# A four-layer graph network: weight tiles regrouped by row chunk, loaded in half as many pieces, and three steps of the start and the end moved

## The chip, the cores and the metric

The kernel runs on one core of one Trainium2 chip. The metric is the device time of that core for one execution, in microseconds. The core has five engines: TensorE (matmuls and transposes; PE in the profile, its weight loads PEld), VectorE (DVE), ScalarE (ACT), GpSimd (POOL) and SyncE (SP), which here only issues transfers.

## The reference

`x` is 128 graphs of 128 nodes with 512 features, `adj` one 128 x 128 weighted adjacency matrix per graph, all in float32. Four layers follow each other, each with a residual and a layer norm:

```
x = norm(x + relu(An x W0 + b0))          An = d (A + I) d,  d = rowsum(A + I)^-1/2
x = norm(x + softmax_nodes(rowsum((q k^T / 8) * A)) * (x Wv^T))    q, k = halves of x Wqk^T
x = norm(x + relu([x, (A x) / rowsum(A)] W2^T))
x = norm(x + An (x W3 + b3))
```

The sums over a row of scores are taken without forming the scores: A k is computed and multiplied by q.

## The kernel before, in words

**Groups and layers.** The 128 graphs go in 32 groups of G = 4. A group `t` keeps its rows in the tile `x_t` (128 nodes x 4 graphs x 512) through all layers; each layer adds into it and normalizes it in place. Rows are named by `r`: r=0 stands for graphs 0 and 2, r=1 for graphs 1 and 3. All matmuls are float32.

**The 512 x 512 products.** `project` (L515 to L578) multiplies a left operand with a weight in seven products of half size instead of eight (Winograd's form of Strassen's method). In the order of TensorE they are B11, B21, T1, T2, B22, T3, T4 (layer 1 has B21 behind T1). B11, B21 use blocks of the left operand as they are; T1, T2, T3, B22 use its four sums s1 to s4 (`left_sums`: s1 is the first and s4 the last; B22 needs s4), in tiles named after the operand with an s behind, so `agg0s`, `xT1s`, `xT2s`. The weight tile holds four blocks and has three of them and the seventh slot turned into weight sums by four subtractions in place (`weight_sums`, L371 to L375). The results are put together by VectorE through `s`, `sb`, `u5`, `u2` (`u_o` and `u_v` in the profile, `s_o` and `s_v` for the copy that ScalarE makes of B11). T4 with what belongs to it is not recorded at once: it is a "tail", which `finish_tails` records, by default behind the B11 of the next `project`, so that the next product covers the waits. `hooks` are functions recorded behind a given product. PSUM has five buffers for these products (`ps_b`) and three for everything else (`ps_t`).

**Left operands.** Layers 0, 2 and 3 need the aggregate of a group transposed, which a matmul gives (`aggregate`, p_agg, copied out by ScalarE as `agg`). Layers 1 and 2 need x itself transposed (`xT`). In the steady state `turn_x` (L465 to L477) does this with DMAs: for each r two transfers into a DRAM scratch (`xT1s<-x`), four back with 32-row blocks exchanged (`xT1y<-xT1s`), and two transposes of 32 x 32 blocks by VectorE, from y into xT. `turn_on_tensor` (L479 to L491) does it with TensorE: for each graph ScalarE copies the rows in another order (into the same y buffers), TensorE transposes four 128 x 128 blocks into a PSUM buffer (`p_xT`), and ScalarE copies them to xT. The adjacency matrices: `prep_rows` (VectorE) makes row sums (`deg`), their powers (GpSimd: `d`) and the two scaled matrices (`ana`: one of x + I by d, one by the row sum); these are transposed on TensorE for groups 0 and 1 (`prep_transpose`; p_a, copied or scaled into `arT` and `anT`), and from group 2 on by DMA through DRAM (`prep_turn`: `sa<-ana`, `ya<-sa`, then VectorE's transposes into `anT`, `arT`).

**Layer 1's small operations.** `l1_qk` gives q and k for two graphs at a time (`p_qk`, copied to `qs`, `kd`), `l1_scores` A k (p_sc) and with VectorE the row sums (`scr`, `w`), `l1_softmax` transposes w (p_w), takes the maximum (`mx`) and exponential (`e`), `l1_weights` transposes back (p_ws). Norms: VectorE's statistics (bn, mv), GpSimd's `rstd` and `mr`, ScalarE's `nmr` and the scaling of x.

**Weights.** `weight` (L356 to L369) loads each of the five 512 x 512 weights (w0, wv, w2x, w2a, w3) into a tile of 128 partitions x (7 slots, 2 row chunks, 256): one transfer for each row half and each column half, so 4 of 256 KB, and with `turned`, where rows are dealt out in four blocks of 32 partitions, 16 of 64 KB.

**The order.** Everything is recorded in a `Plan` (L126 to L268) and issued by `schedule()` (L195 to L258), a list scheduler with a cost model. TensorE keeps the recorded order. VectorE, ScalarE, GpSimd and SyncE take, of what is ready by the model, what is due first, counted back from TensorE. A transfer is 470 ns of SyncE in the model and lands after 1600 ns plus its bytes over a bus. `emit` then issues all; therefore nearly all instructions of the profile stand at L266. All transfers are on SyncE's one queue, in the order of the schedule.

**The sequence.** `begin` (L829 to L851) takes group 0 through layers 0 and 1 and group 1 through layer 0. Its `l0_out(0, ...)` records group 1's adjacency transposes behind B11, and `l1_turn(1)` turns group 1's x by DMA. The main loop (L859 to L877) has, for each t and u = t - 1: l0_out(t), layer 2 of u, l0_agg(t + 1), layer 1 of t, layer 3 of u, with a new group's load and preparation. The period is 76.13 us. Behind the loop (L879 to L886) layers 2 and 3 of the last group are done in two pairs of graphs.

```
        l0_out(0, {B11: [lambda: prep_transpose(1)], B22: [lambda: l0_agg(1)]})
        ...
        l1_turn(1)
        l1_out(0, {B11: [lambda: l1_scores(0)], B21: [lambda: l1_softmax(0)], T3: []})
        finish_tails()
        for r in range(2):
            l1_qk(1, r)
        l2_both(0, 0)
```

Of the kernel before, what the change touches and what calls it, by code (L numbers as in the profile page):

```python
# [15 lines left out]
P = 128  # L16
# [109 lines left out]
class Plan:  # L126
# [4 lines left out]

    ENGINES = ("tensor", "vector", "scalar", "gpsimd", "sync")
    HOP = 200
    LAND, BUS = 1600, 95

    def __init__(self, nc, est):
        self.nc, self.est, self.ops, self.tags, self.group, self.dram = nc, est, [], {}, None, None
# [57 lines left out]
    def schedule(self):  # L195
        number = {op: i for i, op in enumerate(self.ops)}
        for (_, tag, bufs), tiles in self.tags.items():
            used = []
            for t in sorted((t for t in tiles if t.ops), key=lambda t: number[t.ops[0]]):
                if len(used) == bufs:  # L200
                    old = used.pop(min(range(bufs), key=lambda i: number[used[i].ops[-1]]))
                    assert number[old.ops[-1]] < number[t.ops[0]], (tag, bufs)
                    for op in t.ops:
                        if op.preds.isdisjoint(t.ops):
                            op.preds.update(old.ops)
                used.append(t)
        now = 0
        for op in self.ops:
            assert all(number[p] < number[op] for p in op.preds)
            for p in op.preds:  # L210
                p.succs.append(op)
            if op.engine == "tensor":
                op.last = now
                now += op.dur
        for op in reversed(self.ops):
            due = min([s.last - self.hop(op, s) for s in op.succs], default=now)
            op.last = min(op.last, due - op.dur)
        queue = {e: [] for e in self.ENGINES}
        waiting = {op: len(op.preds) for op in self.ops}
        free, bus, port = dict.fromkeys(self.ENGINES, 0), 0, 0  # L220
        pe = [op for op in self.ops if op.engine == "tensor"]
        for op in self.ops:
            if not op.preds:
                queue[op.engine].append((0, number[op], op))
        done = []
        while len(done) < len(self.ops):
            best = None
            for e in self.ENGINES:
                q = queue[e]
                if e == "tensor":  # L230
                    q = [c for c in q if c[2] is pe[0]]
                if not q:
                    continue
                q = [(max(c[0], port if c[2].port else 0),) + c[1:] for c in q]
                at = max(free[e], min(c[0] for c in q))
                pick = min((c for c in q if c[0] <= at), key=lambda c: (c[2].last, c[1]))
                for c in q:
                    if at < c[0] < at + pick[2].dur and c[2].last < at + pick[2].dur and c[2].last < pick[2].last:
                        pick, at = c, c[0]
                if best is None or at < best[0]:  # L240
                    best = at, e, pick[2]
            at, e, op = best
            queue[e] = [c for c in queue[e] if c[2] is not op]
            op.start, op.end = at, at + op.dur
            free[e] = op.end
            if op.port:
                port = op.end
            if e == "sync":
                bus = max(bus, op.end + self.LAND) + op.size / self.BUS
                op.lat = max(op.lat, bus - op.end)  # L250
            if e == "tensor":
                pe.pop(0)
            done.append(op)
            for s in op.succs:
                waiting[s] -= 1
                if not waiting[s]:
                    queue[s.engine].append((max(p.end + self.hop(p, s) for p in s.preds), number[s], s))
        return done  # L258
# [48 lines left out]
def kernel(  # L307
# [48 lines left out]
    def weight(src, name, queue, turned=False):  # L356


        w = const.tile([P, 7, 2, H], FP, tag=name, name=name)
        for h in range(2):  # L360
            for j in range(2):
                s = src[:, j * H:(j + 1) * H]
                if turned:
                    s = s.rearrange("(b h c k) m -> h b k c m", b=Q, h=2, c=2)[h]
                    for b in range(Q):
                        queue.dma_start(w[b * K:(b + 1) * K, 2 * h + j], s[b])
                else:
                    queue.dma_start(w[:, 2 * h + j], s.rearrange("(h c p) m -> h p c m", h=2, c=2)[h])
        return w  # L369

    def weight_sums(w, eng):  # L371
        eng.tensor_tensor(w[:, T3], w[:, B22], w[:, T1], ALU.subtract)
        eng.tensor_tensor(w[:, T1], w[:, T1], w[:, B11], ALU.subtract)
        eng.tensor_tensor(w[:, T2], w[:, B22], w[:, T1], ALU.subtract)
        eng.tensor_tensor(w[:, T4], w[:, B21], w[:, T2], ALU.subtract)  # L375

    def broadcast_row(src, name, queue):
        r = const.tile([P, F], FP, tag=name, name=name)
# [136 lines left out]
    def project(name, t, parts, first, c11, fin, hooks=None, after=lambda: None, early=True,  # L515
# [16 lines left out]
        def product(p, k, fresh):  # L532
            with nc.unit():
                for q in pairs:
                    for i, (left_, w) in enumerate(parts):
                        for c in range(2):
                            nc.tensor.matmul(p[:, q - pairs[0], :], operand(left_, k)[:, q, c, :], w[:, k, c, :],
                                             start=(fresh and q == pairs[0] and i == 0 and c == 0),
                                             stop=(i == len(parts) - 1 and c == 1), skip_group_check=True)
            for f in hooks.get(k, ()):  # L540
                f()
# [93 lines left out]
    def l0_agg(t, eng=nc.gpsimd, pairs=(slice(0, 2),)):  # L635
        left("agg0", t)
        for g in range(G):
            aggregate("agg0", t, g, st["anT", t])
        left_sums("agg0", t, eng, pairs)
# [189 lines left out]
    def begin():  # L829

        prep_rows(0)
        prep_transpose(0)
        weight_sums(w0_sb, nc.gpsimd)
        l0_agg(0, nc.vector, ONE_BY_ONE)
        prep_rows(1)
        l0_out(0, {B11: [lambda: prep_transpose(1)], B22: [lambda: l0_agg(1)]})
        weight_sums(wv_sb, nc.vector)
        l0_out(1)
        l1_turn(0, turn_on_tensor, (0,))
        finish_tails()  # L840
        l1_qk(0, 0)
        l1_turn(0, turn_on_tensor, (1,))
        l1_qk(0, 1)
        for w in (w2x_sb, w2a_sb, w3_sb):
            weight_sums(w, nc.gpsimd)
        l1_turn(1)
        l1_out(0, {B11: [lambda: l1_scores(0)], B21: [lambda: l1_softmax(0)], T3: []})
        finish_tails()
        for r in range(2):
            l1_qk(1, r)  # L850
        l2_both(0, 0)  # L851

    def prep(t):
# [23 lines left out]
            l2_agg(t, 0)  # L877

    l2_both(last, 0)  # L879
    for q in range(2):  # L880
        l2_out(last, {B21: [lambda: l2_both(last, 1)]} if q == 0 else {}, (q,))
    for q in range(2):
        l3_agg_pair(last, q, nc.gpsimd)
        l3_bias(last, (2 * q, 2 * q + 1))
# [34 lines left out]
```

## Time and profile before

| | |
|---|---|
| runs before | 2488.14, 2487.3, 2488.65, 2486.56 us |
| their median | 2487.72 us |
| the profiled execution | 2486.62 us, its span 2484.5 us |
| granted clock of TensorE, mean | 0.997 of full speed |
| bytes moved by DMA | 243.34 MB, mean 98 GB/s |
| loads of x, 1024 KB each | 31, median 5.3 us from issue to landing |
| loads of adj, 256 KB each | 32, median 3.6 us |
| a weight piece of w0, 256 KB | 4, median 6.4 us |

The profile is of one execution and is read in microseconds from the start of its span; the execution's own time is 2.1 us more than the span. Busy shares of the whole span say which engine is used most, and a table of stretches says where that changes. A timeline row is: start, duration, engine, line, operation, output<-inputs, shapes, the number of instructions that it sums up, and in brackets the idle time ahead of it with what ended that. A row of waits is: who waited for whom, total, times, longest. Numbers at the end of a tile's name, or before `_sb`, are left out: w0 and w3 are both `w_sb`. SPq is SyncE's queue: its time is the issuing of a transfer and not the transfer.

### The profile page before, as it was taken

The page shows a single profiled execution, that of the slowest core. Times are in us where ns is not written, and L with a number is a line of the kernel's source. Part 1 is how long each engine was busy: PE and PEld are TensorE (multiplying, and loading weights), DVE is VectorE, ACT ScalarE, POOL GpSimd, SP SyncE. Part 2 cuts the span into 40 slices and gives each one's busy share as a digit, 9 for nine tenths or more (in the row PEclk, how much of TensorE's full clock was granted, in tenths as well). Part 3 has the DMA queues.
Part 4 walks back from the last instruction along what each step waited for, and adds up shares of the span by engine and source line. Part 5 has one row for each costly group of instructions (what it writes and reads, how often), then busy time and mean ns, then how long its engine had stood idle before and what let it go on. Part 6 is the DMA issues. An engine that isn't in the chain of part 4 may idle for free.

```text
span 2484.5 us, 37083 instructions
## 1 busy us (share of the span) xinstructions
PE 2455.6 (99%) x13470; PEld 2205.1 (89%) x13470; DVE 1812.8 (73%) x3169; ACT 972.7 (39%) x1981; POOL 1335.3 (54%) x1522
## 2 busy tenths in 40 slices
PE   8899999999999999999999999999999999999998
PEld 7788988989999899889899998998898999989987
DVE  6777777777777777777777777777777777777665
ACT  3244434443334344343433443433434334443335
POOL 5456555555556465555555564645555555645443
PEclk9999999999999999999999999999999999999999
DMA  5332434433334334344333443243442434433220
GB/s 178 69 100 75 114 90 115 113 82 95 104 100 123 94 81 111 85 123 111 77 102 97 108 123 93 75 112 90 123 111 70 109 90 115 119 82 85 78 59 34
DMA packets 398805, 243.34 MB, mean 98 GB/s; under 512 B 140832, under 2 KB 365600, under 8 KB 398624
## 3 DMA queue, kind: packets, MB, share of 16 engines
q1 hardware_dynamic: 398624, 240.98, 36.4%
q8 instruction: 107, 1.75, 0.3%
q14 instruction: 74, 0.61, 0.1%
HBM read 127.66 MB, written 113.25 MB: 97 GB/s over the span
## 4 chain that ended last, share of the span: by engine, by line
PE 97%; SPq 1%; DVE 1%; DMA 1%; ACT 0%; issue 0%; POOL 0%; ACTq 0%; POOLq 0%; DVEq 0%
PE p_o L266 61%; PE p_v L266 16%; PE p_agg L266 14%; PE p_qk L266 5%; PE p_sc L266 1%; SPq L266 1%; DMA x<-in_x_dram 0%; DVE x L266 0%; PE p_ws L266 0%; ACT xT L266 0%; PE p_w L266 0%; DMA adj<-in_adj_dram 0%; PE p_xT L266 0%; ACT agg L266 0%; DVE wv_sb L266 0%
## 5 line engine op out<-in xcount | busy, mean ns | idle before, releaser
L266 ACT COPY agg<-p_agg 128x512 f32<-128x512 f32 x384 | 220.9, 583 | 572.7 <-PE p_agg L266 572.7
L266 PE MATMUL p_o<-w_sb,agg 128*128 128x256 f32 x1536 | 353.4, 379 | 0.5 <-DVE u_o L266 0.5
L266 PEld LDWEIGHTS p_o<-w_sb,agg 128*128 128x128 f32 x1536 | 286.7, 190 | 37.3 <-DVE u_o L266 0.9
L266 PE MATMUL p_o<-w2x_sb,xT2s 128*128 128x256 f32 x1024 | 263.0, 379 | 3.1 <-DVE xT2s L266 3.1
L266 PE MATMUL p_o<-w2a_sb,agg2s 128*128 128x256 f32 x1024 | 262.8, 379 | 0.0
L266 POOL TENSOR_TENSOR xT1s<-xT 128x512 f32<-128x512 f32 x64 | 94.1, 1471 | 288.0 <-DVE xT L266 190.3
L266 PE MATMUL p_agg<-anT,x 128*128 128x128 f32 x2048 | 243.9, 277 | 0.2 <-DVE anT L266 0.2
L266 PEld LDWEIGHTS p_agg<-anT,x 128*128 128x128 f32 x2048 | 235.4, 192 | 1.2 <-DVE anT L266 0.4
L266 PE MATMUL p_o<-w_sb,agg0s 128*128 128x256 f32 x1024 | 229.1, 381 | 7.2 <-DVE u_o L266 5.9
L266 PE MATMUL p_v<-wv_sb,xT1s 128*128 128x256 f32 x1024 | 233.3, 381 | 0.0
L266 POOL TENSOR_TENSOR agg3s<-agg 128x512 f32<-128x512 f32 x62 | 84.1, 1357 | 271.7 <-ACT agg L266 271.7
L266 PEld LDWEIGHTS p_o<-w_sb,agg0s 128*128 128x128 f32 x1024 | 192.9, 191 | 34.1 <-POOL mro L266 4.9
L266 PEld LDWEIGHTS p_o<-w2x_sb,xT2s 128*128 128x128 f32 x1024 | 194.4, 190 | 29.9 <-DVE xT2s L266 3.6
L266 PE MATMUL p_o<-w_sb,agg3s 128*128 128x256 f32 x992 | 219.2, 379 | 0.0
L266 PEld LDWEIGHTS p_o<-w2a_sb,agg2s 128*128 128x128 f32 x1024 | 194.6, 190 | 26.5
L266 PEld LDWEIGHTS p_v<-wv_sb,xT1s 128*128 128x128 f32 x1024 | 189.6, 190 | 27.3
L266 PEld LDWEIGHTS p_o<-w_sb,agg3s 128*128 128x128 f32 x992 | 188.5, 190 | 25.6
L266 ACT ACTIVATE x<-x,nmro,rstdo 128x512 f32<-128x512 f32 x257 | 198.7, 809 | 4.8 <-ACT nmro L266 0.3
L266 PE MATMUL p_o<-w2x_sb,xT 128*128 128x256 f32 x768 | 197.5, 380 | 1.2 <-ACT s_o L266 0.7
L266 PE MATMUL p_o<-w2a_sb,agg 128*128 128x256 f32 x768 | 197.1, 379 | 0.0
L266 DVE TENSOR_TENSOR u_o<-p_o,s_o 128x512 f32<-128x512 f32 (+1 forms) x132 | 89.1, 675 | 145.3 <-PE p_o L266 145.3
L266 PE MATMUL p_v<-wv_sb,xT 128*128 128x256 f32 x768 | 181.6, 379 | 0.9 <-DVE u_v L266 0.9
(141 smaller groups left out, 4664.1 us busy)
## 6 DMA issues: line engine op xcount, KB each, us to landing
x<-in_x_dram SPq DMA_DIRECT2D x31, 1024.0 KB, 5.3
xT1s<-x SPq DMA_DIRECT2D x124, 256.0 KB, 2.5
xT1y<-xT1s SPq DMA_DIRECT2D x248, 128.0 KB, 3.4
out_dram<-x SPq DMA_DIRECT2D x31, 1024.0 KB, 5.4
xT2s<-x SPq DMA_DIRECT2D x120, 256.0 KB, 2.6
xT2y<-xT2s SPq DMA_DIRECT2D x240, 128.0 KB, 2.9
sa<-ana SPq DMA_DIRECT2D x120, 128.0 KB, 3.3
ya<-sa SPq DMA_DIRECT2D x120, 128.0 KB, 3.3
```

The source lines that it names most:

```text
L266: getattr(getattr(self.nc, op.engine), method)(*[v.real() if isinstance(v, Ref) else v for v in args], **{k: v.real() if isinstance(v, Ref ...
```

## The change

- The weight tile is laid out as 128 partitions x (2 row chunks, 7 slots, 256), so that both column halves of a row half stand side by side and one transfer brings both: 2 transfers of 512 KB instead of 4 of 256 KB, and for `turned` 8 of 128 KB instead of 16 of 64 KB. `weight_sums` and the matmuls index accordingly; a subtraction now covers two runs of 256 elements where it had one run of 512.
- The scheduler's model lets a transfer start only when the ninth transfer before it has landed (FLIGHT). This acts on the planned order; no instruction is added.
- In `begin`, group 1's adjacency transposes are recorded behind B21 of group 0's layer 0 and not behind B11.
- In `begin`, group 1's x is turned by `turn_on_tensor` for layer 1, behind T3 of group 0's layer 1, followed by the first half of group 1's q and k; the second half stays behind the tail.
- At the end, the tail that is pending when layer 2 of the last group begins (T4 of the group before, in layer 3) is taken out of the list and recorded behind `l2_both(last, 1)`, in the B21 hook of the first pair.

```diff
--- before.py
+++ after.py
@@ -131,7 +131,7 @@
 
     ENGINES = ("tensor", "vector", "scalar", "gpsimd", "sync")
     HOP = 200
-    LAND, BUS = 1600, 95
+    LAND, BUS, FLIGHT = 1600, 95, 9
 
     def __init__(self, nc, est):
         self.nc, self.est, self.ops, self.tags, self.group, self.dram = nc, est, [], {}, None, None
@@ -222,7 +222,7 @@
         for op in self.ops:
             if not op.preds:
                 queue[op.engine].append((0, number[op], op))
-        done = []
+        done, landed = [], []
         while len(done) < len(self.ops):
             best = None
             for e in self.ENGINES:
@@ -241,6 +241,8 @@
                     best = at, e, pick[2]
             at, e, op = best
             queue[e] = [c for c in queue[e] if c[2] is not op]
+            if e == "sync" and len(landed) >= self.FLIGHT:
+                at = max(at, landed[-self.FLIGHT])
             op.start, op.end = at, at + op.dur
             free[e] = op.end
             if op.port:
@@ -248,6 +250,7 @@
             if e == "sync":
                 bus = max(bus, op.end + self.LAND) + op.size / self.BUS
                 op.lat = max(op.lat, bus - op.end)
+                landed.append(op.end + op.lat)
             if e == "tensor":
                 pe.pop(0)
             done.append(op)
@@ -356,23 +359,21 @@
     def weight(src, name, queue, turned=False):
 
 
-        w = const.tile([P, 7, 2, H], FP, tag=name, name=name)
+        w = const.tile([P, 2, 7, H], FP, tag=name, name=name)
         for h in range(2):
-            for j in range(2):
-                s = src[:, j * H:(j + 1) * H]
-                if turned:
-                    s = s.rearrange("(b h c k) m -> h b k c m", b=Q, h=2, c=2)[h]
-                    for b in range(Q):
-                        queue.dma_start(w[b * K:(b + 1) * K, 2 * h + j], s[b])
-                else:
-                    queue.dma_start(w[:, 2 * h + j], s.rearrange("(h c p) m -> h p c m", h=2, c=2)[h])
+            to = w[:, :, 2 * h:2 * h + 2].rearrange("p c j m -> p c (j m)")
+            if turned:
+                for b in range(Q):
+                    queue.dma_start(to[b * K:(b + 1) * K], src.rearrange("(b h c k) m -> h b k c m", b=Q, h=2, c=2)[h][b])
+            else:
+                queue.dma_start(to, src.rearrange("(h c p) m -> h p c m", h=2, c=2)[h])
         return w
 
     def weight_sums(w, eng):
-        eng.tensor_tensor(w[:, T3], w[:, B22], w[:, T1], ALU.subtract)
-        eng.tensor_tensor(w[:, T1], w[:, T1], w[:, B11], ALU.subtract)
-        eng.tensor_tensor(w[:, T2], w[:, B22], w[:, T1], ALU.subtract)
-        eng.tensor_tensor(w[:, T4], w[:, B21], w[:, T2], ALU.subtract)
+        eng.tensor_tensor(w[:, :, T3], w[:, :, B22], w[:, :, T1], ALU.subtract)
+        eng.tensor_tensor(w[:, :, T1], w[:, :, T1], w[:, :, B11], ALU.subtract)
+        eng.tensor_tensor(w[:, :, T2], w[:, :, B22], w[:, :, T1], ALU.subtract)
+        eng.tensor_tensor(w[:, :, T4], w[:, :, B21], w[:, :, T2], ALU.subtract)
 
     def broadcast_row(src, name, queue):
         r = const.tile([P, F], FP, tag=name, name=name)
@@ -534,7 +535,7 @@
                 for q in pairs:
                     for i, (left_, w) in enumerate(parts):
                         for c in range(2):
-                            nc.tensor.matmul(p[:, q - pairs[0], :], operand(left_, k)[:, q, c, :], w[:, k, c, :],
+                            nc.tensor.matmul(p[:, q - pairs[0], :], operand(left_, k)[:, q, c, :], w[:, c, k, :],
                                              start=(fresh and q == pairs[0] and i == 0 and c == 0),
                                              stop=(i == len(parts) - 1 and c == 1), skip_group_check=True)
             for f in hooks.get(k, ()):
@@ -833,7 +834,7 @@
         weight_sums(w0_sb, nc.gpsimd)
         l0_agg(0, nc.vector, ONE_BY_ONE)
         prep_rows(1)
-        l0_out(0, {B11: [lambda: prep_transpose(1)], B22: [lambda: l0_agg(1)]})
+        l0_out(0, {B21: [lambda: prep_transpose(1)], B22: [lambda: l0_agg(1)]})
         weight_sums(wv_sb, nc.vector)
         l0_out(1)
         l1_turn(0, turn_on_tensor, (0,))
@@ -843,11 +844,10 @@
         l1_qk(0, 1)
         for w in (w2x_sb, w2a_sb, w3_sb):
             weight_sums(w, nc.gpsimd)
-        l1_turn(1)
-        l1_out(0, {B11: [lambda: l1_scores(0)], B21: [lambda: l1_softmax(0)], T3: []})
+        l1_out(0, {B11: [lambda: l1_scores(0)], B21: [lambda: l1_softmax(0)],
+                   T3: [lambda: l1_turn(1, turn_on_tensor), lambda: l1_qk(1, 0)]})
         finish_tails()
-        for r in range(2):
-            l1_qk(1, r)
+        l1_qk(1, 1)
         l2_both(0, 0)
 
     def prep(t):
@@ -877,8 +877,9 @@
             l2_agg(t, 0)
 
     l2_both(last, 0)
+    held = tails.pop()
     for q in range(2):
-        l2_out(last, {B21: [lambda: l2_both(last, 1)]} if q == 0 else {}, (q,))
+        l2_out(last, {B21: [lambda: l2_both(last, 1), held]} if q == 0 else {}, (q,))
     for q in range(2):
         l3_agg_pair(last, q, nc.gpsimd)
         l3_bias(last, (2 * q, 2 * q + 1))
```

## The prediction

> **What bounds the kernel now.** I read the page's busy shares first, then a table of busy time by stretch, then TensorE's waits in the first stretch.
>
> ```profile
> span 2484.5 us, 37083 instructions
> ...
> PE 2455.6 (99%) x13470; PEld 2205.1 (89%) x13470; DVE 1812.8 (73%) x3169; ACT 972.7 (39%) x1981; POOL 1335.3 (54%) x1522
> ```
>
> ```profile
> 0.00:100.00 100.00, 82.81 (x466) 72.19 (x467) 70.83 (x121) 31.90 (x61) 55.34 (x60) 0.97 0.50 145
> 100.00:2420.00 2320.00, 2320.00 (x12729) 2086.79 (x12728) 1705.78 (x2976) 905.84 (x1844) 1260.11 (x1420) 1.00 0.37 98
> 2420.00:2485.00 65.00, 52.81 (x279) 46.10 (x277) 36.21 (x74) 34.94 (x76) 19.85 (x43) 0.95 0.09 33
> ```
>
> After the stretch and its length, the first number is TensorE's busy time. Between 100 and 2420 us it never waits, so there nothing can be gained without taking matmuls away; other engines there matter only if they become late. Idle are 17.2 us in the first 100 and 12.2 us at the end, where 9 us follow the last matmul. The first stretch's waits:
>
> ```profile
> PE p_o L266 <- DVE u_o L266: 5.9, 2, 4.5
> PE p_qk L266 <- DVE xT L266: 3.4, 1, 3.4
> ...
> PE p_o L266 <- DVE xT2s L266: 1.5, 1, 1.5
> ...
> PE p_o L266 <- POOL agg0s L266: 1.2, 1, 1.2
> ```
>
> TensorE's timeline has two of them, each with slow matmuls behind it:
>
> ```profile
> 36.34 3.74 PE L266 MATMUL p_o<-w_sb,agg0s 128*128 128x256 f32 x16 [1.15 <-POOL agg0s L266]
> 44.61 5.38 PE L266 MATMUL p_o<-w_sb,agg0s 128*128 128x256 f32 x16 [4.53 <-DVE u_o L266]
> ...
> 75.44 5.44 PE L266 MATMUL p_qk<-wqk_sb,xT 128*128 128x128 f32 x32 [3.36 <-DVE xT L266]
> ```
>
> The same 16 records take 3.74 us and then 5.38. By the starts of the rows behind them, 44.61 and 75.44 lose 1.7 us each besides the wait. What made VectorE and GpSimd late stands in their timelines and in SP's:
>
> ```profile
> 35.26 0.69 DVE L266 TENSOR_REDUCE deg<-adj 128x4 f32<-128x512 f32 x1 [4.52 <-DMA adj<-in_adj_dram]
> ...
> 31.52 1.27 POOL L266 TENSOR_TENSOR w2a_sb<-w2a_sb 128x512 f32<-128x512 f32 x1 [11.61 <-DMA w2a_sb<-in_L_gnn_W_dram]
> ...
> 28.39 3.75 SPq L266 DMA_DIRECT2D w2x_sb<-in_L_gnn_W_dram x8
> ...
> 32.26 0.38 SPq L266 DMA_DIRECT2D adj<-in_adj_dram  x1
> ```
>
> Both stand in front of group 1's work and wait for transfers behind SP's long row of weight pieces.
>
> **What the Trainium skill says.** "DMA: Bandwidth & Descriptors", Rules for kernel authors: many small transfers should be coalesced into one large one. The trace agrees here: in SP's issuing order 33 weight issues between 16.17 and 32.26 us take 0.49 us each, pieces of 64 KB among them, while the DMA engines were often not full. "SBUF — State Buffer", SBUF: two separate sides: a VectorE operation with two SBUF inputs and a GpSimd one exclude each other for a whole instruction. It agrees: `ana<-adj,ident` takes 0.66 us without GpSimd at work and 1.70 beside it. "TensorE: Matmul & The Clock Gate", What's actually happening: after an idle window (about 3.4 us) the clock is halved for about as long. The lost 1.7 us behind the waits of 4.53 and 3.36 us agree; behind 1.15 us nothing is lost.
>
> **The change part by part.**
>
> *Weights in half as many pieces, order on SP.* Same bytes. An issue waits, by SP's waits, for the transfer some eight before it: x of group 1 lands at 15.80 (5.93 + 9.87 in the chain) and holds SP. What is ahead of it in bytes stays, so I leave 15.8. Behind it come 5 + 2 + 8 weight issues instead of 33: 15 x 0.49 = 7.3, so adj of group 2 is issued at 23.2 and, with its 2.98 us of before, lands at 26.2 instead of 35.2. VectorE comes to `deg` at 25.4 and waits 0.8 to 2 instead of 4.52; the last W2 piece lands near 25, so GpSimd's W2 sums end by 28 and group 1's sums start when ScalarE's copy is there (28.9). Sum s1 is ready at 30.2 (needed 35.1), s4 at 35.5 (needed 38.7); VectorE reaches the u5 sum that holds B22 at 37.4 (needed 38.7). So 1.15 + 4.53 + 1.7 = 7.4 go; I leave 0.3 for small waits: gain 7.1.
>
> *Group 1's adjacency transposes behind B21 instead of B11, group 0's sums before `ana`.* B21 then follows B11 at once but must wait for ScalarE's copy of the block (ends 14.51, B11 ends 13.73): 0.8, in place of the 0.81 wait for `ana`. VectorE has the same operations against the same five GpSimd ones of 1.44, so B22 starts where it did (22.7). I book a loss of 0.2, between -1 and +0.6.
>
> *Layer 1 of group 1 on TensorE.* Added: 16 transposes, 2 x 1.04 = 2.1 us of TensorE (row `p_xT` x8), and on ScalarE four copies into xT1y (0.56 each) and four back (0.54). Gone: 12 transfers, four VectorE transposes (2.49) and the wait of 3.36 with its 1.7. Of the rest of this stretch (49.8 to 96.1) 0.24 + 0.85 + 0.29 + 0.68 + 1.51 of waits go too, in all 8.6; new ones come:
> - ScalarE has a copy of p_xT ahead of the last xT1y: 0.3.
> - T4 must wait for the u5 sum, now behind the statistics of rows r=0 on VectorE: weights at 61.6, then 0.16 + 0.47 + about 2 + 0.47 + 1.27 + 0.3 + 0.69 make 66.7, TensorE is there at 65.5: 1.2.
> - Layer 2 of group 0 begins without the slack that the wait gave: a PSUM buffer for p_xT becomes free only after `kd` and `qs` (0.6), the copy of xT (0.35), the s_o copy (0.7).
> - VectorE now has `anT<-ya` of group 2 ahead of group 0's layer-2 sums. In the trace ya lands 9 us after `ana` ends (85.4 to about 94.4); `ana` would end near 75.5, ya lands near 84.5, and four operations later T1 can start at 87.4 against 85.6 by TensorE alone: 1.8.
>
> Sum 2.1 + 0.3 + 1.2 + 1.65 + 1.8 = 7.0, gain 8.6 - 7.0 = 1.6.
>
> *Weight sums on two runs of 256 instead of 512.* No row of before has this form; its elements are the same, so 0. At 0.3 us more each, the 20 sums lie beside TensorE's work: 0 still, at most 0.5 loss at the start.
>
> *T4 of group 30 held back to the end of B21's hooks.* Before, TensorE waits 1.57 for `xT2s` after the p_xT there. T4's 1.73 us of matmuls (2429.50 to 2431.23) fill it. Between B11 and B21, where T4 stood, the s_o copy is bare: 0.65. Gain 0.9. Group 30's store comes some 5 us later than 2444, before group 31's rows are stored, so the last transfer does not move. Between 0 and 1.5.
>
> *At most nine in flight.* This limits only the planner's clock; no wait is added on the chip. It alters orders. The order lists of both programs differ at the start, in groups 2 to 10 and at the end; in groups 11 to 29 they are the same, so those keep 76.13 us each. In groups 2 to 10 the x store goes ahead of the second four xT1y loads, `anT` moves behind the statistics, those of layer 2 go ahead of the second transposes, and `deg` goes ahead of `scr`. The last is the tight one; by the timelines of one group, before:
>
> ```profile
> 1030.75 0.85 SPq L266 DMA_DIRECT2D adj<-in_adj_dram  x1
> ...
> 1033.41 0.42 DVE L266 TENSOR_TENSOR scr<-p_sc,qs 128x256 f32<-128x256 f32 x1 [1.34 <-PE p_sc L266]
> ...
> 1036.49 0.68 DVE L266 TENSOR_REDUCE deg<-adj 128x4 f32<-128x512 f32 x1
> ...
> 1036.65 0.27 PE L266 MATMUL p_w<-ident,w 128*4 128x128 f32 x1
> ```
>
> adj lands 3.5 us after its issue, 1034.25. `deg` in front makes `scr` start at 1034.95 and w be ready at 1036.0 (0.42 + 0.45 + 0.16), 0.6 before `p_w` needs it. Everything behind waits with it (mx, e, then p_ws, which had 2.5 us). Now when does adj land after the change? Its transfers follow `ana`, and that the second transposes. Their data, with 1 MB of store ahead (some 2.6 us at the 400 GB/s seen then) but an earlier start of the row, I put at 1020.0; VectorE is free at 1020.85 (u5). From their end at 1022.1, x and three `ana` alternate with GpSimd's sums (1.68 a pair, from 1.13 + 0.55) and end at 1027.8, before at 1027.9. So adj is no later. Cost 0, at most 0.5 us a group if the store shifts the loads by its whole 2.6; I take 0.05 x 9 = 0.5 in all.
>
> **Sum.** 7.1 - 0.2 + 1.6 + 0.9 - 0.5 = 8.9, say 9.0 us less than the profiled execution's 2486.62 (span 2484.5 and 2.1 around it): 2477.6. The median of the runs shown, 2487.72, is 1.1 above that execution; against it the forecast is 2478.7.
>
> **Rivals.**
> 1. *The start only exchanges its waits.* The pieces may be limited by data and not by issues: 2.6 MB from 15.5 us on at the 350 GB/s of before end at 23 anyway, and with some landings late adj comes at 29, not 26.2; VectorE's chain is then 3 us late against a slack of 1.3 at B22 (1.7 lost, and 0 or 1.7 for the clock), and the norm of x for layer 2 slips 2 more. Gain 3 to 4, with the end: 2484. For it: the DMA was at 9 tenths until 15 us. Against: behind 15 us it moved 100 to 200 GB/s.
> 2. *Groups 2 to 10 wait for adj (slower).* If adj lands 2.6 us later than before (the store's whole time), `p_w` is 2.0 late in each of nine groups, 18 us, against 9.5 gained: 2496. It decides from 1.05 us a group, so from a landing 1.65 later. For it: a slack of only 0.6 and two engines excluding each other in between. Against: the loads have 1.6 us of room behind u5, and their row of issues starts earlier.
> 3. *More goes than I book*: x of layer 2 and ya come in time, 4 us more: 2474.7.
>
> **How the numbers follow.** Forecast 0.62 (own range 2475 to 2482), rival 1 0.18, rival 2 0.14, rival 3 0.06. The bound for no change, 0.2%, is 5 us, about what a measurement tells. Faster: forecast, rival 3: 0.66 with rounding to rival 1's edge; same 0.21, of rival 1 and of mild forms of rival 2; slower 0.13. The range 2474 to 2488 leaves out rival 2's upper part and little below.
>
> **What would show it.** TensorE's start rows: no wait above 1.5 at the B22 of group 1 and at `p_qk`; `deg` of group 2 before 28 us; T1 of group 0's layer 2 near 87.5, not 96.11; groups 11 to 29 at 76.13; in groups 2 to 10 `p_w` without a wait. I am wrong if a wait `p_w` from w stands there nine times, if `deg` is still near 35, or if the 16-record row at B22 still takes over 5 us.

## The result: 0.14% slower, where 0.36% faster was forecast

The changed kernel takes 2491.11 us as a median of 42 runs (2487.0 to 2495.18), the kernel before 2487.82 us. The ratio is 1.0014 with a 95% interval of 1.001 to 1.0019. The profiled execution took 2490.21 us, its span is 2488.4 us, 3.9 us more than before.

The page after, its first line and the busy shares, and the table of stretches (length, then busy time of TensorE, its weight loads, VectorE, ScalarE, GpSimd, then clock, DMA share, GB/s):

```profile
span 2488.4 us, 37039 instructions
...
PE 2459.1 (99%) x13486; PEld 2207.5 (89%) x13486; DVE 1810.5 (73%) x3165; ACT 976.8 (39%) x1989; POOL 1338.6 (54%) x1522
```

```profile
0.00:100.00 100.00, 84.58 (x478) 74.22 (x479) 69.39 (x118) 36.02 (x69) 58.11 (x60) 0.95 0.43 124
100.00:2420.00 2320.00, 2316.54 (x12710) 2082.94 (x12709) 1701.37 (x2970) 905.66 (x1844) 1256.42 (x1416) 1.00 0.37 98
```

In the first 100 us TensorE idles 15.4 us, not much less than the 17.2 before, at a mean clock of 0.95 for 0.97, and the long middle has 3.46 us of idle time where it had none. Its waits over the whole span (total, times, longest) name both:

```profile
PE p_o L269 <- DVE u_o L269: 8.0, 4, 5.7
PE p_w L269 <- DVE rs L269: 3.4, 3, 1.2
PE p_o L269 <- DVE xT2s L269: 2.8, 1, 2.8
```

In the timeline they have their places, and here the slow matmuls behind two of them are seen too:

```profile
37.62 5.27 PE L269 MATMUL p_o<-w_sb,agg 128*128 128x256 f32 x16 [5.73 <-DVE u_o L269]
...
95.40 2.08 PE L269 MATMUL p_o<-w2x_sb,xT2s 128*128 128x256 f32 x4 [2.84 <-DVE xT2s L269]
97.27 1.80 PE L269 MATMUL p_o<-w2a_sb,agg2s 128*128 128x256 f32 x4
...
353.88 0.27 PE L269 MATMUL p_w<-ident,w 128*4 128x128 f32 x1 [1.03 <-DVE rs L269]
...
583.64 0.27 PE L269 MATMUL p_w<-ident,w 128*4 128x128 f32 x1 [1.22 <-DVE rs L269]
...
813.34 0.27 PE L269 MATMUL p_w<-ident,w 128*4 128x128 f32 x1 [1.17 <-DVE rs L269]
```

The first is T4 of group 0's layer 0, which waited for nothing before. The start rows of TensorE in the two profiles give the account, stage by stage:

| TensorE starts | before | after | gained since the row above | forecast |
|---|---|---|---|---|
| B22 of group 0, layer 0 | 22.71 | 22.87 | -0.16 | -0.2 |
| second half of p_qk, group 0 | 55.66 | 55.87 | -0.05 | 7.1 |
| T1 of group 0, layer 2 | 96.11 | 95.40 | 0.92 | 1.6 |
| p_w of group 1 | 123.13 | 124.10 | -1.68 | 0 |
| p_w of group 10 | 808.27 | 813.34 | -4.10 | -0.5 |
| p_w of group 31 | 2403.31 | 2408.38 | 0 | 0 |
| last four matmuls | 2475.32 | 2479.39 | 1.00 | 0.9 |

The sum is -4.07; another 0.17 us is gained behind the last matmul, which gives the 3.9 us of the spans. Two rows carry most of the error: the start, where a gain of 7.1 did not come, and groups 2 to 10, which lost 4.1. A third part, 2.4 us, lies around layer 2 of group 0: 0.92 for 1.6 ahead of it and -1.68 for 0 behind it.

What stands behind the first is in VectorE's timeline, with SyncE's issue of the transfer:

```profile
26.67 0.39 SPq L269 DMA_DIRECT2D adj<-in_adj_dram  x1
...
24.90 0.69 DVE L269 TENSOR_TENSOR u_o<-p_o,u_o 128x512 f32<-128x512 f32 x1 [0.82 <-PE p_o L269]
31.86 0.69 DVE L269 TENSOR_REDUCE deg<-adj 128x4 f32<-128x512 f32 x1 [6.26 <-DMA adj<-in_adj_dram]
...
32.95 3.21 DVE L269 SCALAR_TENSOR_TENSOR x<-u_o,x 128x512 f32<-128x512 f32 x2
36.19 0.69 DVE L269 BATCH_NORM_STATS2 bno<-x 128x6 f32<-128x512 f32 x1
36.80 0.67 DVE L269 TENSOR_TENSOR u_o<-p_o,u_o 128x512 f32<-128x512 f32 x1
```

VectorE stands 6.26 us on the row sum of group 2, which nobody needs yet, and group 0's x, its statistics and the u5 sum (36.80) queue behind it. u5 reads the PSUM buffer into which T4 accumulates, so T4 starts at 37.62. In the kernel before the same sum was done at 30.05, ahead of `deg`, and T4 ran in one row with the products ahead of it, without a wait; by the timelines of TensorE and VectorE of the kernel before:

```profile
29.85 5.34 PE L266 MATMUL p_o<-w_sb,agg 128*128 128x256 f32 x24
...
30.05 0.69 DVE L266 TENSOR_TENSOR u_o<-p_o,u_o 128x512 f32<-128x512 f32 x1 [1.87 <-PE p_o L266]
```

So adj is used 3.4 us earlier than before (31.86 against 35.26), and more than that is lost because the planner, believing it earlier still, put `deg` in front. In the plan's own time, as each kernel computes it, adj of group 2 lands at 22.58 in the changed kernel and at 26.66 in the kernel before; that puts `deg` at 24.28, ahead of the u5 sum (28.66), where it stood at 28.56, behind that sum (27.87).

In group 4 the same thing happens in small. `deg` of group 7, which is prepared there, waits for adj; `scr` stands behind it, and so the scores of group 4 are late. By the timelines of SyncE and VectorE:

```profile
344.47 2.83 SPq L269 DMA_DIRECT2D sa<-ana  x4
347.34 0.80 SPq L269 DMA_DIRECT2D adj<-in_adj_dram  x1
...
352.06 0.69 DVE L269 TENSOR_REDUCE deg<-adj 128x4 f32<-128x512 f32 x1 [3.19 <-DMA adj<-in_adj_dram]
352.67 0.41 DVE L269 TENSOR_TENSOR scr<-p_sc,qs 128x256 f32<-128x256 f32 x1
```

A table of 2 us stretches, with the DMA share and GB/s at the end:

```profile
346.00:348.00 2.00, 2.00 (x14) 1.84 (x14) 1.97 (x3) 0.75 (x3) 1.92 (x2) 1.00 0.95 141
348.00:350.00 2.00, 2.00 (x15) 1.87 (x14) 0.87 (x4) 0.58 (x1) 1.40 (x3) 1.00 0.93 191
```

adj is there 4.7 us after its issue, and the DMA engines are 0.95 busy at only 141 GB/s. The four strip stores `sa` of `ana` stand ahead of adj in every group, so they are not what sets group 4 apart; what does is told under "Groups 2 to 10" below.

### The profile page after: what moved, and what is told of

Read it like the earlier page. It is cut to its first block, busy times and chain, and to the rows that moved or that the text cites. A ratio compares the mean times of both kernels' runs of the same rounds, so it can differ in the third digit from the quotient of the medians.

```text
span 2488.4 us, 37039 instructions
## 1 busy us (share of the span) xinstructions
PE 2459.1 (99%) x13486; PEld 2207.5 (89%) x13486; DVE 1810.5 (73%) x3165; ACT 976.8 (39%) x1989; POOL 1338.6 (54%) x1522
## 4 chain that ended last, share of the span: by engine, by line
PE 94%; DMA 2%; DVE 2%; SPq 1%; ACT 0%; POOL 0%; issue 0%; ACTq 0%; POOLq 0%; DVEq 0%
PE p_o L269 60%; PE p_v L269 15%; PE p_agg L269 13%; PE p_qk L269 4%; PE p_sc L269 1%; SPq L269 1%; DMA adj<-in_adj_dram 1%; DVE x L269 1%; DMA x<-in_x_dram 0%; DVE ana L269 0%; DMA xT1s<-x 0%; DMA xT1y<-xT1s 0%; DMA w2a_sb<-in_L_gnn_W_dram 0%; PE p_ws L269 0%; POOL rstdo L269 0%
```

## The experiments

All are told against the kernel before in the same runs (medians of 2487.56 to 2488.29); 2491.11 is the changed kernel. Several of them alter only the planned order: a dependency inside the plan between two operations of one engine, which adds no wait on the chip. Runs 2, 6 and 10 move only a few VectorE operations by it (run 2 also one of GpSimd). In runs 1 and 3 the planner besides returns to the order of the kernel before in the later groups, with `deg` behind `scr`. The edits stand in `schedule()` in front of `now = 0`, where `by` finds an operation by the first tile of that name which it writes, and `wrote` the last one.

One question needed no run. Built without the limit of nine (`FLIGHT`), the changed kernel has the same order of instructions on all five engines, row for row. So the limit contributes nothing here, and the orders that the prediction put down to it have another source.

**1. deg of group 2 behind u5.**

```diff
+        by["deg_2"].preds.add(wrote["u5_o0_0"])
```

> The changed kernel, with one planned order altered: VectorE may take the row sum deg of group 2 only behind group 0's u5 sum of layer 0 (a dependency in the plan alone; transfers are issued in the same order as in the changed kernel at the start). Theory A (VectorE stands on adj of group 2 for 6.3 us with group 0's u5 behind it, so T4 of group 0 is 5.7 us late and 1.6 us more go with the slow clock behind it): T4 starts near 31.8 instead of 37.62, no 16-record row over 5 us there, and the start of layer 1 (first p_qk, 52.81 in the changed kernel) comes 5 to 7 us earlier. By the order list deg then also stands behind scr in groups 5 and later, so the p_w waits (3.4 in all) go too: together 2478 to 2481. Rival B (the transfers as such are late, whatever the order): the wait moves from T4 to B22 of group 1, where the kernel before has 4.5, the clock is slow there again, and p_qk comes no more than 1.5 us earlier: 2486 to 2488.

Measured: 2480.59 us (ratio 0.997, 0.996 to 0.9981). TensorE and VectorE, by their timelines:

```profile
29.31 5.34 PE L274 MATMUL p_o<-w_sb,agg 128*128 128x256 f32 x24
35.64 3.72 PE L274 MATMUL p_o<-w_sb,agg0s 128*128 128x256 f32 x16 [0.98 <-POOL agg0s L274]
42.17 5.16 PE L274 MATMUL p_o<-w_sb,agg0s 128*128 128x256 f32 x16 [2.82 <-POOL rstdo L274]
...
29.51 0.69 DVE L274 TENSOR_TENSOR u_o<-p_o,u_o 128x512 f32<-128x512 f32 x1 [1.87 <-PE p_o L274]
31.91 0.69 DVE L274 TENSOR_REDUCE deg<-adj 128x4 f32<-128x512 f32 x1 [1.71 <-DMA adj<-in_adj_dram]
```

adj lands when it did (31.91), but T4 follows B11 without a wait: it is in the first row of 24. Part of it comes back as a wait of 2.82 at B22 with a slow row behind it; the second half of p_qk starts at 53.00, 2.9 us earlier than in the changed kernel, less than the 5 to 7 expected. The named releaser there is not the real one: B22 goes into the buffer that VectorE's u5 of group 1 reads until 42.02. Theory A holds for T4, rival B for about half of the size. The later groups have no p_w wait, since their order is that of the kernel before: group 10's p_w comes 7.49 us earlier, 3.4 of them gained up to the p_w of group 1 (120.70 against 124.10) and 4.1 in groups 2 to 10. (The profiled execution is the slowest of its eight, 2.1 us above the median.)

**2. deg of the later groups behind scr.**

```diff
+        for t in range(4, 32):
+            by["vector", f"deg_{t}"].preds.add(by["vector", f"scr_{t - 3}"])
```

> The changed kernel, with deg of group t planned behind scr of group t - 3 for t from 4 on (plan only); all transfers stay in the changed kernel's order, and the start is untouched. Theory A (deg in front of scr waits for adj, and with it the scores): the three p_w waits of 1.0 to 1.2 go, groups 1 to 10 have the period of 76.13, and the time falls by 3.4 to 4 us, to about 2487. Rival B (the store ahead of the second x loads and the later anT make these groups late): p_w or something near it still waits, and the time stays within 1 us of 2491.

Measured: 2487.55 us (0.9998, 0.9989 to 1.0007), 3.6 less than the changed kernel. From the p_w of group 1 (125.45) to that of group 10 (810.64) it takes 685.19 us; the kernel before takes 685.14 and the changed kernel 689.24. The store ahead of the loads and the other exchanged rows are still there, so rival B falls. The loss of 4.1 us in groups 2 to 10 is that one order.

**3. adj of group 2 first.**

```diff
+            if op.engine == "sync" and isinstance(op.calls[0][1][0], Ref) and op.calls[0][1][0].tile.args[3]["name"] in ('adj_2',):
+                op.last = -1
```

(in the loop that sets the due times)

> The changed kernel, with one transfer moved: adj of group 2 is issued ahead of the pieces of wv and w2 instead of behind them. Theory A (it is late because 2.6 MB of weights stand ahead of it and have to be moved first): deg of group 2 is done by 17 us, T4 of group 0 and B22 of group 1 have no wait over 1.5, 6 to 8 us go before the first p_qk; deg is behind scr in the later groups here too by the order list, so 3.4 more: 2477 to 2481. Rival B (GpSimd is the later one: it waits until 31.4 for the last w2 piece with group 1's left sums behind it): s1 to s4 come when they came, B22 waits 3 us or more, and less than half of it is gained: 2484 to 2487.

Measured: 2480.97 us (0.9972, 0.996 to 0.9984).

```profile
10.14 0.38 SPq L271 DMA_DIRECT2D adj<-in_adj_dram  x1
...
19.00 0.69 DVE L271 TENSOR_REDUCE deg<-adj 128x4 f32<-128x512 f32 x1 [1.34 <-DMA adj<-in_adj_dram]
...
32.66 5.34 PE L271 MATMUL p_o<-w_sb,agg 128*128 128x256 f32 x24
37.84 3.62 PE L271 MATMUL p_o<-w_sb,agg0s 128*128 128x256 f32 x16
41.79 3.69 PE L271 MATMUL p_o<-w_sb,agg0s 128*128 128x256 f32 x16 [0.33 <-DVE u_o L271]
```

T4, s1 and B22 have no wait to speak of, and no slow row. deg comes at 19.0, later than the 17 expected. GpSimd still starts its first W2 sum at 31.45, so rival B was wrong to see GpSimd as the limit. The plan of the very first operations changed as well: B22 of group 0 starts at 25.53, 2.7 us later than in the changed kernel, which eats a part of the gain.

**4. Group 1's x turned by DMA again**, the rest as changed: the lines of `l1_turn(1)` as before.

> The changed kernel without its third part: group 1's x for layer 1 is turned by DMA as before. By the order list deg stands behind scr again from group 5 on. Theory A (this part, not the limit of nine transfers, set deg in front of scr): no p_w waits; T4 of group 0 still waits 5.7; p_qk of group 1 waits 3 to 4 again with a slow clock behind; the start of T1 in group 0's layer 2 comes 0 to 3 us later than 95.40. In sum 2486 to 2490. Rival B (the limit of nine did it): p_w still waits three times and the time is 2491 or more.

Measured: 2486.6 us (0.9995, 0.9986 to 1.0003). No p_w waits; T4 waits 7.11; the old wait is back, with its slow clock:

```profile
76.55 5.44 PE L269 MATMUL p_qk<-wqk_sb,xT 128*128 128x128 f32 x32 [3.41 <-DVE xT L269]
```

So the transposes on TensorE do what they are for, and taking them out is still 4.5 us faster than the changed kernel, since the later groups keep their order. It isn't this part alone that decides about that order: with it kept, runs 1 and 3 have it right too. A shift in the planned start can decide on which side of `scr` a `deg` falls.

**5. The turned weights over all partitions**: four transfers of 128 partitions for wv and w2x each.

```diff
-                for b in range(Q):
-                    queue.dma_start(to[b * K:(b + 1) * K], src.rearrange("(b h c k) m -> h b k c m", b=Q, h=2, c=2)[h][b])
+                for c in range(2):
+                    queue.dma_start(to[:, c], src.rearrange("(b h c k) m -> h c b k m", b=Q, h=2, c=2)[h, c])
```

> The changed kernel, with the turned weights (wv, w2x) loaded in four transfers of 256 KB over all 128 partitions instead of eight of 128 KB over 32 partitions each: the same bytes to the same places. Theory A (pieces over 32 partitions move at some 100 GB/s, whatever their number: 8 x 128 KB take 10.2 us in the changed kernel and 16 x 64 KB 11.4 us in the one before): the row of wv issues falls below 6 us, GpSimd's first w2 sum starts by 27 instead of 31.43, deg of group 2 before 28 instead of 31.86, T4 of group 0 waits 2 us or less instead of 5.73; the three p_w waits stay, since the order stays: 2483 to 2487. Rival B (the bytes of all weights set it): the w2 sum still starts at 30 to 32, T4 waits 5 or more, 2490 to 2492.

Measured: 2505.19 us (1.0071, 1.0056 to 1.0086). A miss for both: the timelines of SyncE, VectorE and TensorE and the table of stretches show a start that is far slower.

```profile
17.31 6.29 SPq L269 DMA_DIRECT2D w2x_sb<-in_L_gnn_W_dram  x2
...
45.40 0.69 DVE L269 TENSOR_REDUCE deg<-adj 128x4 f32<-128x512 f32 x1 [20.08 <-DMA adj<-in_adj_dram]
...
51.16 6.00 PE L269 MATMUL p_o<-w_sb,agg 128*128 128x256 f32 x16 [19.55 <-DVE u_o L269]
```

```profile
22.00:26.00 4.00, 3.41 (x23) 3.21 (x24) 2.49 (x5) 0.49 (x1) 0.00 (x0) 1.00 0.26 100
```

The DMA engines are 0.26 busy in that stretch, and two issues of w2x take 6.29 us. The records of single packets show why it is slow: between 22 and 26 us only four packets of 2 KB are under way at a time, 84 ns each, which makes the 100 GB/s of that line; in the changed kernel 16 or more are under way at a time from 24 us on. The source of such a transfer has its four row blocks outermost. That this number sets the four was not tested by a run. (The rates that the expectation starts from, 10.2 and 11.4 us, are no rates of the pieces: 4.1 and 3.3 us of them are SyncE's wait for x of group 1.) What the run does show is how far the effect of one landing goes: adj comes 13.5 us later, T4 is 13.5 us later (51.16 against 37.62), the time grows by 14.1.

**6. anT of group 2 behind the layer 2 sums.**

```diff
+        by["anT_2"].preds.update((by["xT2s4_0"], by["agg2s4_0"]))
```

> The changed kernel, with group 2's anT planned behind group 0's layer 2 sums s1, s2, s4 on VectorE (plan only). Theory A (anT waits for ya and stands in front of the sums): T1 of group 0's layer 2 waits 1.0 to 1.6 instead of 2.84, and its first rows are no longer at half clock (1.8 us): 2.5 to 3.2 us less, about 2488. Rival B (the sums wait for ScalarE's copies of agg and xT anyhow): T1 waits 2.2 or more, nothing or less than 1 us is gained.

Measured: 2490.07 us (1.0009, 1.0001 to 1.0018). T1 waits 2.33 and its first rows are still slow: rival B by number. But the timeline shows `arT<-ya`, not moved, in front of the sums in its place, waiting for the same ya until 93.07. Run 10 moves both.

**7. The new weight tiles alone**, on the kernel before.

> The kernel before with the first part alone: the weight tiles by row chunk and half as many transfers. Theory A (fewer pieces change when the planner believes adj of group 2 to be there, so that deg moves in front of group 0's x and u5; the landing itself moves by some 3 us only): T4 of group 0 waits 5 to 7 us where the kernel before waits 0 there, in exchange for its 1.15 and 4.53 behind; no p_w waits; 2486 to 2490, no gain. Rival B (as forecast, issues are what holds adj back): adj lands near 26, T4 waits less than 1.5, and 5 to 7 us are gained: 2481 to 2483.

Measured: 2487.84 us (1.0, 0.9991 to 1.0008). T4 waits 6.99, adj is issued at 26.57 and deg starts at 32.38. Theory A; the gain that the prediction hung on this part isn't there.

**8. The held tail alone**, on the kernel before.

> The kernel before with the last part alone: T4 of group 30 recorded behind the B21 hooks of the last group's layer 2. Theory A: TensorE's last matmul group starts 0.9 to 1.1 us earlier than 2475.32, and the time falls by the same: about 2486.8. Rival B (the store of group 30, 5 us later, delays the rows of group 31): the matmuls end earlier but the time does not fall.

Measured: 2487.12 us (0.9997, 0.9988 to 1.0006), too small for the times. In the timeline the group 31 p_w starts 0.32 us later than before (2403.63) and the last matmuls 0.68 earlier, so the part is worth 1.00 us:

```profile
2474.64 1.13 PE L266 MATMUL p_o<-w_sb,agg 128*128 128x256 f32 x4 [0.52 <-DVE u_o L266]
```

**9. Runs 2, 3 and 10 together** on the changed kernel.

> The changed kernel with three repairs together: adj of group 2 issued ahead of wv's pieces (as in the third run), deg of group t planned behind scr of group t - 3 from t = 4 on, and group 2's anT and arT both planned behind group 0's layer 2 sums. Theory A (the three places are all there was): no p_w waits, T1 of group 0's layer 2 starts by 90.2 with a wait below 1.4, the span falls below 2478; 2477 to 2480 as a median. Rival B (the sums wait for ScalarE's copy of xT, not for VectorE): T1 starts at 90.5 as in the third run, and the time is that run's, 2481, within 0.5.

Measured: 2480.35 us (0.9972, 0.9961 to 0.9982). T1 starts at 90.86 with a wait of 1.50; before it VectorE waits for ScalarE's copies of agg and xT and no longer for ya. That is rival B in time: no more than run 3.

**10. anT and arT behind the sums.**

```diff
+        s = (by["xT2s4_0"], by["agg2s4_0"])
+        by["anT_2"].preds.update(s)
+        by["arT_2"].preds.update(s)
```

> The changed kernel with group 2's anT and arT both planned behind group 0's layer 2 sums (the run with anT alone left arT in front of them). Theory A (VectorE's two transposes, which wait for ya, hold the sums): T1 waits 1.2 to 1.8 instead of 2.84 and 2.33, its first rows run at full clock, and against the changed kernel 2.5 to 3 us go by group 1's p_w. Rival B (agg and xT are copied too late by ScalarE): T1 still waits 2.2 or more.

Measured: 2487.95 us (1.0003, 0.9995 to 1.0011), 3.2 less than the changed kernel.

```profile
96.11 1.13 PE L276 MATMUL p_o<-w2x_sb,xT2s 128*128 128x256 f32 x4 [1.51 <-DVE xT2s L276]
97.08 1.03 PE L276 MATMUL p_o<-w2a_sb,agg2s 128*128 128x256 f32 x4
```

The wait is 1.51, as in the kernel before, and the rows are at full speed. From the second half of p_qk (57.90) to group 1's p_w (123.13) it takes 65.23 us, in the changed kernel 68.23: 3.0 less. Theory A. The kernel before takes 67.47 for that stretch, so with the order mended the turning on TensorE is worth 2.2 us there.

**11 and 12. Old and new weight tiles with the repaired orders.** Both have the kernel before's place of group 1's adjacency transposes, the TensorE transposes, the held tail and the edits of run 9; 12 has the new tiles as well.

> The kernel before with everything of the run of all repairs except the new weight tiles, the place of group 1's adjacency transposes and the limit of nine: TensorE transposes for group 1's layer 1, the tail of group 30 held back, adj of group 2 first, deg behind scr, anT and arT behind the sums. Theory A (the number of weight pieces gives little once adj of group 2 doesn't stand behind them): within 2 us of the run of all repairs, 2478 to 2482. Rival B (33 issues instead of 15 hold back the last w2 piece, and GpSimd with it): s1 or B22 of group 1 waits 3 us or more, 2482 to 2485.

> As the run before, with the new weight tiles added. Theory A: the last w2 piece comes at most 2.5 us earlier, and the time within 1.5 us of the run before and of the run of all repairs. Rival B: 2 to 5 us faster than the run before.

Measured: 2480.24 us (0.9972, 0.9962 to 0.9983) and 2480.49 us (0.9976, 0.9969 to 0.9983). With the old pieces GpSimd gets the last W2 piece later:

```profile
34.09 3.17 POOL L277 TENSOR_TENSOR w2a_sb<-w2a_sb 128x512 f32<-128x512 f32 x2 [8.74 <-DMA w2x_sb<-in_L_gnn_W_dram]
```

(31.45 in run 9), and TensorE doesn't feel it: 0.80 at s1 and 0.41 at B22. The weight tiles give nothing that can be measured. Run 12's executions form two groups, ten of 2478.68 to 2480.49 us and eight of 2482.13 to 2485.64, where run 11's reach from 2479.0 to 2482.5; the profiled one of run 12 (2485.01) is of the second group and has three spells of half clock in the start. What parts the groups stays open. The best versions, runs 1, 3, 9, 11 and 12, lie within 0.8 us of each other, about 7.4 us below the kernel before; the cheapest of them is run 1, one more line in the plan of the changed kernel.

## Why the prediction was wrong

**The landing of adj (failed).** "15 x 0.49 = 7.3, so adj of group 2 is issued at 23.2 and, with its 2.98 us of before, lands at 26.2." It was issued at 26.67 and used at 31.86, 5.7 us later than that. By SyncE's timeline and its waits:

```profile
17.10 3.49 SPq L269 DMA_DIRECT2D wv_sb<-in_L_gnn_W_v_dram  x5
...
SPq L269 <- DMA x<-in_x_dram: 4.3, 2, 4.1
SPq L269 <- DMA w2a_sb<-in_L_gnn_W_dram: 2.4, 2, 1.3
```

All three terms were too short. SyncE goes on behind its wait for x at 17.10 and not at 15.8 (1.3 us). The fifteen issues behind it take 9.6 us and not 7.3 (2.2): most take about 0.47, but one takes 1.72 and one waits 1.3 for a piece of w2a. From issue to use adj takes 5.2 us and not 2.98 (2.2). The table of stretches, after and before, shows how full the way was:

```profile
24.00:32.00 8.00, 7.89 (x52) 7.02 (x51) 0.91 (x3) 2.42 (x5) 0.57 (x1) 1.00 1.08 292
...
24.00:32.00 8.00, 8.00 (x54) 7.46 (x53) 4.08 (x8) 2.57 (x5) 0.47 (x1) 1.00 0.74 211
```

The DMA engines have no time left while adj is under way, at 292 GB/s, so the bytes ahead of it set its landing more than the number of issues does; run 3, with adj ahead of them, uses it at 19.00. This is the prediction's first rival, which saw the direction, with 29. Run 7 repeats the landing with the weight tiles alone (issued at 26.57, used at 32.38). What should have followed fell too: GpSimd's two W2 sums, to end by 28, started at 31.43 (31.52 before) and ended at 33.9.

**What stands behind deg (left out).** The prediction let VectorE reach `deg` at 25.4 and did not name what it had passed: x, the statistics and u5 of group 0, with T4 waiting for u5. So the waits of 1.15 and 4.53 did go, as forecast, and 5.73 with 1.65 of slow clock came in T4's place. Run 1 shows it: adj lands as late, but T4 waits for nothing and the p_w of group 1 comes 3.4 us earlier; the rest of its gain (2480.59) comes from the order of the later groups.

**Groups 2 to 10 (cost forecast at 0.5, measured 4.1).** The second rival had the mechanism and the place, `deg` in front of `scr` with 0.6 us of slack, but charged 2.0 us to nine groups where three lost 1.2 to 1.4. The failing step is "So adj is no later": it looked at when adj can be issued and took 3.5 us for the way. In groups 4, 7 and 10 it took 4.7 to 4.9 us, in the other six 3.5 to 3.6. Those three are the ones in which a packet of 16 KB of the queue that the profile calls "instruction" starts while adj is under way, at 349.3, 578.9 and 808.8 us (the profile's list of DMA queues has 107 such packets). Over all the traces, 296 loads of adj behind 150 us met no such packet and took 3.1 to 4.0 us; 61 met one, and all 46 that took more than 4.4 us (up to 5.5) are among these. In run 6 the packet came too late for adj of group 10 (3.56 us), and no p_w waited there. In the kernel before the load in group 4 takes 4.98 us and does no harm, with `deg` behind `scr`. No run moves these packets, so their part is a correlation; that the order of `deg` and `scr` turns the late load into lost time is shown by run 2. The cause named for the order, the limit of nine, was wrong: it changes nothing. The changed kernel also scatters more: its 42 runs span 8.2 us, the 12 of run 2 3.4.

**Layer 1 on TensorE (1.6 forecast, 0.92 measured, and 1.68 lost behind it).** The added rows and ScalarE's 0.32 are as booked, the wait of T4 for u5 is 1.07 for 1.2 (the terms that the prediction lists there add up to 67.0 and not 66.7, so by its own sum it was 1.5). The term that was mis-sized is T1 of layer 2: 2.84 for 1.8, and a wait of that length slowed the rows behind it. The prediction let `ana` end near 75.5 without saying what stands ahead of it; it ended at 83.4, behind the layer 1 statistics in VectorE's order. Then `deg` of group 3 waited for adj until 90.15 and anT for ya until 92.70, both in front of the sums:

```profile
90.15 0.69 DVE L269 TENSOR_REDUCE deg<-adj 128x4 f32<-128x512 f32 x1 [6.75 <-DMA adj<-in_adj_dram]
...
92.70 0.71 DVE L269 STREAM_TRANSPOSE anT<-ya 128x512 f32<-128x512 f32 x1 [0.77 <-DMA ya<-sa]
```

Run 10 removes this part.

**Right:** the place of group 1's adjacency transposes (-0.16 for -0.2), the held tail (1.00 for 0.9), the weight sums on two runs of 256 (1.26 us, against 1.27 before), 76.13 us for groups 11 to 29.

## What to carry to other kernels

In a planned order, an operation that waits for a transfer takes all behind it on its in-order engine along: when a change makes the planner believe a transfer earlier, look at what that transfer's reader has overtaken before counting what the earlier landing may save. Fewer transfers of the same bytes moved a landing by 3.4 us here, where the count of issues promised 9, with the DMA engines full. If one wants data early, its transfer has to stand ahead of the bulk in the queue, or its reader behind what is urgent.

## What the runs showed of the hardware

- The clock of TensorE changes on a fixed grid of 3.41 us. Spells of half clock start on it and last whole steps: in the changed kernel from 33.98 to 40.80, two steps, and from 95.42 to 98.83, one, 18 steps after the first start. In these traces the idle time inside one step decides, and not the length of a wait. Over all the traces, each of the 22 full-clock steps in which TensorE was idle for 0.61 of the step or more was followed by a step of half clock, and none of the 10,028 with 0.55 or less was; of two between, at 0.56 and 0.57, the first was and the second was not. So a wait of 2.64 us in run 3, which lies across two steps, cost nothing (3.84 us for 32 matmuls of p_agg), and one of 2.40 at the same place in run 9, inside one step, slowed them to 5.47. Each row of the table is one step; run 3 first, then run 9:

```profile
6.70:10.11 3.41, 1.82 (x15) 1.34 (x13) 0.72 (x2) 0.58 (x1) 0.41 (x1) 1.00 1.02 351
10.11:13.53 3.42, 1.91 (x17) 1.91 (x18) 3.24 (x7) 0.59 (x1) 2.48 (x2) 1.00 1.05 369
...
8.82:12.23 3.41, 1.01 (x10) 0.89 (x9) 2.28 (x6) 0.59 (x1) 1.46 (x2) 1.00 0.95 327
12.23:15.64 3.41, 3.41 (x19) 3.41 (x18) 3.38 (x3) 1.17 (x2) 3.25 (x3) 0.50 1.14 287
```

TensorE is idle for 0.47 and 0.44 of run 3's two steps and for 0.70 of run 9's first, and run 9's next step is at 0.50 of the clock. Likewise, behind 2.84 us before layer 2 of the changed kernel two groups of rows took 2.08 and 1.80 us for about 1.03, behind 2.33 in run 6 1.64 and 1.91, and behind 1.51 in run 10 there was no loss. The Trainium skill, "TensorE: Matmul & The Clock Gate", What's actually happening, has a window of about 3.4 us and calls it free-running; the traces agree with both. They differ from its idle window in one thing: a step that was idle for somewhat more than half was enough.
- The Trainium skill, "DMA: Bandwidth & Descriptors", Rules for kernel authors, advises to coalesce many small transfers into one large. Here half as many pieces of the same bytes brought adj 3.4 us earlier, with the DMA engines full (1.08 at 292 GB/s), and with the repaired orders the old and the new pieces give the same time (2480.24 and 2480.49 us). Run 5 is no example against the advice: its larger pieces are slow while only four packets at a time are under way.
